# Thirty-two unrolled batch tiles rewritten as a hardware loop of eight iterations, in a kernel that stores at the DMA limit

## The chip, the cores and the metric

The kernel runs on one core of one Trainium2 chip. The metric is the device time of one execution in microseconds (us), given as the median of several runs. One execution of each kernel also leaves a trace; its span is the time from the first to the last recorded instruction, 1.8 us less than that execution's device time in the kernel before (1339.7 against 1341.49 us).

## The reference

A batch of 4096 rows, each of 32 fields of 64 numbers. For each of the 496 pairs of fields (i < j), field i goes through the pair's own 64x64 matrix and is multiplied by field j, element by element. The output has 4096 x 31,744 fp32 numbers, 520 MB.

```python
i_idx, j_idx = np.triu_indices(32, k=1)
vi = inputs[:, i_idx, :]                     # inputs (4096, 32, 64)
vj = inputs[:, j_idx, :]
vdotw = jnp.einsum('bpd,pde->bpe', vi, W)    # W (496, 64, 64)
return (vdotw * vj).reshape(4096, -1)
```

## The kernel before

A batch tile is 128 rows, one on each partition. Its x is loaded and transposed on TensorE (PE), so that a field's 64 numbers lie on partitions and PE loads them as weights ahead of the matmuls with that field's matrices (the trace has 4,864 such loads of 64x128, 194 ns each, and as many matmuls of 64x512 or less, 559 ns each on average). The products of PE land in one of four PSUM slots; VectorE (DVE) multiplies them by x and writes the result into a ring in SBUF; SyncE (SP) issues one store for each of five groups of fields. The weights stay in SBUF. The 32 batch tiles are unrolled by a Python loop, so each instruction is executed once.

```python
STORES = [[0, 1], [2, 3], [4, 5], [6, 7, 8], [9, 10, 11, 12, 13, 14, 15]]
PREFETCH_AT = [5, 6]
RING = 28160
...
for p in range(NPR):                          # 16 loads of weights, issued by SP
    wp = const.tile([P, width[2 * p]], F32, tag=f"w{p}", name=f"w{p}")
    nc.sync.dma_start(out=wp, in_=w[:, woff[p] : woff[p] + width[2 * p]])
    w_sb.append(wp)
... # transpose x of tile 0
for t in range(NT):                           # 32 batch tiles
    xt, xT = xs.pop(t), xTs.pop(t)
    if t + 1 < NT:
        xs[t + 1] = load_x(t + 1)             # issued by ACT
    for s, group in enumerate(STORES):
        if at + store_w[s] > RING:
            at = 0
        osb = ring[:, at : at + store_w[s]]
        at += store_w[s]
        for p in group:
            ... # transposes of the next x tile at p = 5 and 6
            for c0 in range(0, width[2 * p], BANK):
                pm = psum.tile([P, 2, BANK], F32, tag="ps")        # 4 slots in turn
                ... # two matmuls into pm, then one or two DVE products into osb
        nc.sync.dma_start(out=out[ts(t, P), o0 : o0 + store_w[s]], in_=osb)
```

## Time and profile before

| | before |
|---|---|
| time | 1341.44 us (1341.24 to 1341.58, in the rounds with the changed kernel) |
| span, instructions executed | 1339.7 us, 13,755 |
| DMA | 9 in all slices but the last, 420 GB/s over the span |
| DVE, PE busy | 88%, 86% |
| DVE's first product, first store issued | 13.16 us, 24.61 us |

The lines that carry this stand in the prediction. In the page a digit is the busy share of one of 40 slices in tenths; a queue's line gives packets, megabytes and share of sixteen DMA engines; a line of the waits gives who waits for whom, microseconds in total, how often, and the longest.

### The profile page before, as it was taken

How to read it: one execution, taken by the hardware profiler on the slowest of the kernel's cores; microseconds unless marked ns; L12 is line 12 of the kernel's file. 1: busy time of each engine (PE TensorE's matmuls, PEld its weight loads, DVE VectorE, ACT ScalarE, POOL GpSimd, SP SyncE). 2: the span in 40 equal slices, each digit the busy share in tenths (PEclk: the TensorE clock that was granted, in tenths of full speed). 3: DMA queues.
4: the chain of work that ended last, by engine and by line, in shares of the span. 5: the costliest groups of instructions: out<-in, count | busy, mean ns of one | idle time of the engine just before them, and what ended most of it. 6: DMA issues, size and time to landing. Idle time of an engine off the chain costs nothing.

```text
span 1339.7 us, 13755 instructions
## 1 busy us (share of the span) xinstructions
PE 1151.0 (86%) x5376; PEld 548.7 (41%) x5376; DVE 1177.4 (88%) x1664; ACT 66.1 (5%) x65; POOL 0.7 (0%) x6
## 2 busy tenths in 40 slices
PE   7998889888898888988888978889798897888992
PEld 3444344443343443443433534444344443444441
DVE  6999889888899988989888989899898997898993
ACT  1000000000000000000000000000000000000000
POOL 0000000000000000000000000000000000000000
PEclk9999889999999999989999899899898998998996
DMA  9999999999999999999999999999999999999996
GB/s 392 426 431 434 429 431 429 427 427 434 426 434 430 422 422 430 422 424 429 415 426 424 426 426 404 415 420 431 428 420 408 431 427 431 416 424 420 422 429 264
DMA packets 30017, 562.93 MB, mean 420 GB/s; under 512 B 3456, under 2 KB 3840, under 8 KB 5376
## 3 DMA queue, kind: packets, MB, share of 16 engines
q1 hardware_dynamic: 25344, 528.49, 92.6%
q10 hardware_dynamic: 4608, 33.56, 6.0%
q8 instruction: 42, 0.69, 0.2%
q14 instruction: 23, 0.19, 0.0%
HBM read 41.94 MB, written 520.09 MB: 420 GB/s over the span
## 4 chain that ended last, share of the span: by engine, by line
DMA 54%; DVE 23%; PE 11%; issue 9%; DVEq 0%
DMA out_dram<-ring 54%; DVE ring L130 15%; PE pm L120 9%; DVE ring L139 9%; PE pt L80 2%; DMA x<-in_x_dram 1%; DVEq L130 0%; DVEq L177 0%
## 5 line engine op out<-in xcount | busy, mean ns | idle before, releaser
L120 PE MATMUL pm<-w,xT 64*128 64x512 f32 (+7 forms) x4864 | 1083.2, 559 | 158.3 <-DVE ring L130 140.1
L130 DVE TENSOR_TENSOR ring<-pm,x 128x1024 f32<-128x1024 f32 x768 | 904.0, 1217 | 138.4 <-DMA out_dram<-ring 93.0
L120 PEld LDWEIGHTS pm<-w,xT 64*128 64x128 f32 x4864 | 487.7, 194 | 720.1 <-DVE ring L130 451.3
L139 DVE TENSOR_TENSOR ring<-pm,x 128x448 f32<-128x448 f32 (+6 forms) x896 | 330.2, 415 | 3.6 <-PE pm L120 2.9
L81 ACT COPY xT<-pt 128x1024 f32<-128x1024 f32 x64 | 64.8, 1012 | 1194.6 <-PE pt L80 1194.6
L80 PE MATMUL pt<-ident,x 128*128 128x128 f32 x512 | 76.5, 297 | 8.5 <-DMA x<-in_x_dram 8.5
L80 PEld LDWEIGHTS pt<-ident,x 128*128 128x128 f32 x512 | 61.0, 152 | 48.9 <-issue 35.3
L81 ACT ACT_TABLE_LOAD x1 | 1.3, 1283 | 1.7 <-PEq L173 1.7
masks.py:199 POOL TENSOR_SCALAR_AFFINE_SELECT ident<-ident 128x128 f32<-128x128 f32 x1 | 0.3, 292 | 0.1
masks.py:197 POOL MEMSET ident<- 128x128 f32 x1 | 0.2, 204 | 0.3 <-POOLq L173 0.3
L173 POOL MEMSET const-bfloat16-1.0<- 128x1 bf16 x1 | 0.1, 101 | 0.0
L173 POOL MEMSET const-uint8-127<- 128x1 uint8 x1 | 0.1, 101 | 0.0
L173 POOL MEMSET const-float32-0.0<- 128x1 f32 x1 | 0.1, 98 | 0.2 <-issue 0.2
L173 POOL MEMSET const-float32-1.0<- 128x1 f32 x1 | 0.1, 98 | 0.0
## 6 DMA issues: line engine op xcount, KB each, us to landing
out_dram<-ring SPq DMA_DIRECT2D x32, 3776.0 KB, 22.8
out_dram<-ring SPq DMA_DIRECT2D x32, 3264.0 KB, 21.8
out_dram<-ring SPq DMA_DIRECT2D x32, 3168.0 KB, 22.4
out_dram<-ring SPq DMA_DIRECT2D x32, 2912.0 KB, 22.3
out_dram<-ring SPq DMA_DIRECT2D x32, 2752.0 KB, 22.1
x<-in_x_dram ACTq DMA_DIRECT2D x32, 1024.0 KB, 14.2
w<-in_w_dram SPq DMA_DIRECT2D x1, 992.0 KB, 7.4
w<-in_w_dram SPq DMA_DIRECT2D x1, 928.0 KB, 11.7
```

Source lines behind the costliest of these rows:

```text
L80: nc.tensor.transpose(pt[:, ts(c, P)], xt[:, ts(n * g + c, P)], ident)
L81: nc.scalar.copy(xT[:, ts(g, 2 * BANK)], pt)
L120: nc.tensor.matmul(pm[:, h, : n[h]], xT[h * D : (h + 1) * D, ts(p, P)], w_sb[p][h * D : (h + 1) * D, c0 : c0 + n[h]], start=True, stop=True,)
L130: nc.vector.tensor_tensor(runs(osb, o[0], o[1], n[0]), pm[:, :, : n[0]], runs(xt, xj[0], xj[1], n[0]), ALU.mult,)
L139: nc.vector.tensor_tensor(osb[:, o[h] : o[h] + n[h]], pm[:, h, : n[h]], xt[:, xj[h] : xj[h] + n[h]], ALU.mult,)
L173: nc = bacc.Bacc("TRN2", target_bir_lowering=False, num_devices=1)
```

## The change

The intent is a smaller program: instead of 32 unrolled tiles, eight iterations of four (the prediction says why four). The loop is built with `iteration_sync="reg_based"`: by that name its waits compare with registers, and the trace of the changed kernel has 1,328 register operations on PE and 1,384 on DVE, where the kernel before has none. Stores are declared disjoint, so that rows held in registers create no dependence between them. The last iteration prefetches one x tile too many, for which x gets 128 rows of zeros.

```diff
-RING = 28160
+RING = 26272
+BODY = 4
...
-    psum = ctx.enter_context(tc.tile_pool(name="ps", bufs=4, space=bass.MemoryType.PSUM))
+    pspool = ctx.enter_context(tc.tile_pool(name="ps", bufs=1, space=bass.MemoryType.PSUM))
...
+    xbuf = [const.tile([P, F * D], F32, tag=f"x{k}", name=f"x{k}") for k in range(2)]
+    xTbuf = [const.tile([P, NPR * P], F32, tag=f"xT{k}", name=f"xT{k}") for k in range(2)]
+    slots = [
+        pspool.tile([P, 2, BANK], F32, tag=f"ps{k}", name=f"ps{k}") for k in range(4)
+    ]
...
-    for t in range(NT):
-        xt, xT = xs.pop(t), xTs.pop(t)
-        if t + 1 < NT:
-            xs[t + 1] = load_x(t + 1)
+    def batch_tile(row, k, nxt):
+
+        xt, xT = xbuf[k], xTbuf[k]
+        load_x(nxt, 1 - k)
...
-            nc.sync.dma_start(out=out[ts(t, P), o0 : o0 + store_w[s]], in_=osb)
+            st = nc.sync.dma_start(out=out[bass.ds(row, P), o0 : o0 + store_w[s]], in_=osb)
+
+            tc.declare_no_dep(
+                st.ins, group="stores", across_iterations=True, reason="disjoint outputs"
+            )
+            tc.add_to_no_dep_group("stores", st.ins)
+
+    first_slot = turn["slot"]
+    with tc.For_i(0, B, BODY * P, iteration_sync="reg_based") as r:
+        for j in range(BODY):
+            batch_tile(r + j * P, j % 2, r + (j + 1) * P)
...
+    x = np.concatenate([x, np.zeros((P, F * D), x.dtype)])
```

More of the change, by code (lines that the diff above doesn't have):

```diff
@@ L47, in pair_bilinear_kernel @@
     nc = tc.nc
-    B = x.shape[0]
+    B = out.shape[0]
     NT = B // P
@@ L57, in pair_bilinear_kernel, with slot @@
     const = ctx.enter_context(tc.tile_pool(name="const", bufs=1))
-    xpool = ctx.enter_context(tc.tile_pool(name="x", bufs=2))
-    xtpool = ctx.enter_context(tc.tile_pool(name="xT", bufs=2))
-    psum = ctx.enter_context(tc.tile_pool(name="ps", bufs=4, space=bass.MemoryType.PSUM))
+    pspool = ctx.enter_context(tc.tile_pool(name="ps", bufs=1, space=bass.MemoryType.PSUM))
     ident = const.tile([P, P], F32, tag="ident", name="ident")
     make_identity(nc, ident)
+    ring = const.tile([P, RING], F32, tag="ring", name="ring")
+    xbuf = [const.tile([P, F * D], F32, tag=f"x{k}", name=f"x{k}") for k in range(2)]
[3 more added lines that the diff above has]
+    ]
+    turn = {"slot": 0, "at": 0}
+    def slot():
+        turn["slot"] = (turn["slot"] + 1) % 4
+        return slots[turn["slot"]]
     def runs(tl, a, b, n):
@@ L68, in runs, with load_x, transpose_x @@
         return bass.AP(ap.tensor, ap.offset, [list(ap.ap[0]), [b - a, 2], list(ap.ap[1])])
-    def load_x(t):
-        xt = xpool.tile([P, F * D], F32, tag="x", name=f"x_{t}")
-        nc.scalar.dma_start(out=xt, in_=x[ts(t, P), :])
-        return xt
-    def transpose_x(xT, t, xt, g):
+    def load_x(row, k):
+        nc.scalar.dma_start(out=xbuf[k], in_=x[bass.ds(row, P), :])
+    def transpose_x(k, g):
         n = 2 * BANK // P
-        pt = psum.tile([P, 2 * BANK], F32, tag="ps", name=f"pt_{t}_{g}")
+        pt = slot().rearrange("p a b -> p (a b)")
         for c in range(n):
-            nc.tensor.transpose(pt[:, ts(c, P)], xt[:, ts(n * g + c, P)], ident)
-        nc.scalar.copy(xT[:, ts(g, 2 * BANK)], pt)
-    def new_xT(t):
-        return xtpool.tile([P, NPR * P], F32, tag="xT", name=f"xT_{t}")
-    ring = const.tile([P, RING], F32, tag="ring", name="ring")
-    at = 0
-    xs = {0: load_x(0)}
+            nc.tensor.transpose(pt[:, ts(c, P)], xbuf[k][:, ts(n * g + c, P)], ident)
+        nc.scalar.copy(xTbuf[k][:, ts(g, 2 * BANK)], pt)
+    load_x(0, 0)
     w_sb = []
@@ L94, in pair_bilinear_kernel @@
         w_sb.append(wp)
-    xTs = {0: new_xT(0)}
     for g in range(2):
-        transpose_x(xTs[0], 0, xs[0], g)
-    for t in range(NT):
-        xt, xT = xs.pop(t), xTs.pop(t)
-        if t + 1 < NT:
-            xs[t + 1] = load_x(t + 1)
+        transpose_x(0, g)
+    def batch_tile(row, k, nxt):
+        xt, xT = xbuf[k], xTbuf[k]
+        load_x(nxt, 1 - k)
         for s, group in enumerate(STORES):
-            if at + store_w[s] > RING:
-                at = 0
-            osb = ring[:, at : at + store_w[s]]
-            at += store_w[s]
+            if turn["at"] + store_w[s] > RING:
+                turn["at"] = 0
+            osb = ring[:, turn["at"] : turn["at"] + store_w[s]]
+            turn["at"] += store_w[s]
             o0 = off[2 * group[0]]
             for p in group:
-                if t + 1 < NT and p in PREFETCH_AT:
-                    if t + 1 not in xTs:
-                        xTs[t + 1] = new_xT(t + 1)
-                    transpose_x(xTs[t + 1], t + 1, xs[t + 1], PREFETCH_AT.index(p))
+                if p in PREFETCH_AT:
+                    transpose_x(1 - k, PREFETCH_AT.index(p))
                 for c0 in range(0, width[2 * p], BANK):
-                    pm = psum.tile([P, 2, BANK], F32, tag="ps", name=f"pm_{t}_{p}_{c0}")
+                    pm = slot()
                     n = [max(0, min(BANK, width[2 * p + h] - c0)) for h in range(2)]
@@ L144, in pair_bilinear_kernel @@
                                 )
-            nc.sync.dma_start(out=out[ts(t, P), o0 : o0 + store_w[s]], in_=osb)
+            st = nc.sync.dma_start(out=out[bass.ds(row, P), o0 : o0 + store_w[s]], in_=osb)
[7 more added lines that the diff above has]
+            batch_tile(r + j * P, j % 2, r + (j + 1) * P)
+    assert turn["slot"] == first_slot and turn["at"] + store_w[0] > RING and BODY % 2 == 0
 def kernel(r_inputs, L0_rec_W):
```

## The prediction

The forecast came to 1350 us: 1341.3 + 2.5 (step 3) + 7.5 (step 6) = 1351, and about 1 less for fewer fetches.

> **What bounds the kernel now.** I read the page from the top: the engines, the 40 slices, the DMA queues and the chain. Then I read the waits, the engines in short stretches at both ends, and the groups of instructions.
>
> ```profile
> span 1339.7 us, 13755 instructions
> ...
> PE 1151.0 (86%) x5376; PEld 548.7 (41%) x5376; DVE 1177.4 (88%) x1664; ACT 66.1 (5%) x65; POOL 0.7 (0%) x6
> ...
> DMA  9999999999999999999999999999999999999996
> GB/s 392 426 431 434 429 431 429 427 427 434 426 434 430 422 422 430 422 424 429 415 426 424 426 426 404 415 420 431 428 420 408 431 427 431 416 424 420 422 429 264
> DMA packets 30017, 562.93 MB, mean 420 GB/s; under 512 B 3456, under 2 KB 3840, under 8 KB 5376
> ...
> q1 hardware_dynamic: 25344, 528.49, 92.6%
> q10 hardware_dynamic: 4608, 33.56, 6.0%
> q8 instruction: 42, 0.69, 0.2%
> q14 instruction: 23, 0.19, 0.0%
> ```
>
> No engine is full, but the DMA row is full in 39 of 40 slices, and the queues add up to 98.8% of sixteen engines' span. So bytes set the time. A tile stores 31,744 fp32 words on each of 128 partitions (16.25 MB) and loads 1.05 MB of x, 17.30 MB in all. Without the first and last slice the mean rate is (420 x 40 - 392 - 264) / 38 = 424.8 GB/s, so a tile costs 17.30 MB / 424.8 GB/s = **40.7 us of DMA**.
>
> The groups and the waits show how close the next engine is:
>
> ```profile
> L130 DVE TENSOR_TENSOR ring<-pm,x 128x1024 f32<-128x1024 f32 x768 | 904.0, 1217 | 138.4 <-DMA out_dram<-ring 93.0
> L139 DVE TENSOR_TENSOR ring<-pm,x 128x448 f32<-128x448 f32 (+6 forms) x896 | 330.2, 415 | 3.6 <-PE pm L120 2.9
> ```
> ```profile
> DVE ring L130 <- DMA out_dram<-ring: 93.0, 53, 3.3
> DVE ring L130 <- PE pm L120: 45.4, 52, 13.2
> ```
>
> DVE has 1177.4 / 32 = **36.8 us a tile** and PE 36.0. DVE's longest wait in total, 93.0 us in 53 pieces (2.9 us a tile), is for a store to leave the ring: the consumer holds up the producer, as behind a full pipe. DVE thus has 40.7 - 36.8 = 3.9 us a tile to spare. The second kind of slack is the backlog. A store lands 22.4 us (median) after its issue, while a mean store of 3.25 MB needs 3.25 / 424.8 = 7.7 us of DMA; so about 22.4 - 7.7 = **14.7 us of other transfers** stand ahead of it. A pause of DVE shorter than that doesn't empty the queue.
>
> The ends, in the stretches (microseconds, busy time and count of PE, PEld, DVE, ACT, POOL, clock, DMA share, GB/s):
>
> ```profile
> 0.00:10.00 10.00, 1.53 (x8) 1.56 (x9) 0.00 (x0) 1.28 (x1) 0.70 (x6) 1.00 0.83 316
> 10.00:20.00 10.00, 9.86 (x48) 5.57 (x47) 6.84 (x8) 2.02 (x2) 0.00 (x0) 1.00 1.01 419
> 20.00:30.00 10.00, 9.27 (x38) 3.12 (x38) 10.00 (x13) 0.00 (x0) 0.00 (x0) 1.00 1.05 413
> ```
>
> DMA is full from the first microseconds, first with weights and x, then with stores. The timeline has the first DVE product at 13.16 us and the first store issued at 24.61 us, just when the 8.4 MB of weights and two x tiles, (8.39 + 2.10) / 0.42 = 25 us of DMA, run out. This handover is the fragile place.
>
> [...] 0.88 MB of fetches are 0.2% of DMA time and stop nothing. [...] the trace shows separate waits of 21 ns in DVE's sequencer, hidden under products of 1217 ns.
>
> **The change part by part.**
>
> 1. *Ring 28160 to 26272.* I walked the allocation. Groups are 7552, 6528, 5504, 6336 and 5824 words. With wrap-around at 28160 no group ever ends above 26272, and the positions repeat every four tiles: tile 4 starts at 0 again. So the two rings are identical, with the same 3 or 4 stores between a slot's use and its reuse, and this costs **0**. It is also why the body has four tiles. PSUM keeps four slots in turn: 42 a tile, 168 an iteration, a multiple of four.
>
> 2. *Compute, stores, x loads.* Per tile the same matmuls, products and 5 stores. Declaring stores disjoint only prevents a dependence that register-held rows would create; the unrolled kernel had none. **0**.
>
> 3. *One x tile more.* The last body prefetches the zero padding: 1.05 MB / 424.8 GB/s = **+2.5 us**, on the bound resource. Its 16 transposes (16 x 0.15 us of PE) fit beside other work.
>
> 4. *Register work.* I expect about one register instruction per wait. DVE's sequencer now handles 1664 products and 750 separate waits, 75 a tile. [...] **0** on the path. [...]
>
> 5. *Seven back edges.* [...] For a fetch under load I take the smallest weight load as an upper estimate: 32 KB landed 5.3 us after issue. [...] A pause of 5 us is below the 14.7 us backlog and is earned back within two tiles (3.9 us each). All seven, if exposed, would be 35 us; I count **0**.
>
> 6. *Loop entry.* Straight code lets PE begin when the first weights are in. A loop may instead make each engine wait, before entering, for everything loaded earlier that the body uses. Weights are issued until 0.73 + 22.97 = 23.7 us and the last lands 5.3 us later, at about 29 us. DVE would start about 2.7 us after (13.16 us less the end of the first transposed copy at about 10.5), near 31.5 instead of 13.2, and the first store would go out 11.45 us later, at 43 instead of 24.6. DMA would run dry from about 27 to 43 us, **+15 us**, never regained because DMA is the bound. I give this one chance in two: +7.5 us.
>
> Sum: 1341.3 + 2.5 + 7.5 = 1351; a small credit for fewer fetches (0.88 MB is at most 2.1 us) makes it 1350.
>
> **The rivals.** *A: hidden loop, no entry wait.* For it: the ring waits and the backlog. Time about 1344 us. *B: entry wait.* For it: the first store comes just when loads run out. Against it: waits against the first weight's semaphore could stay in the body. Time about 1359 us. *C: DVE or PE becomes the bound*, by exposed register work on every wait or by coarser waits across the back edge. For it: a margin of only 3.9 us a tile, and DVE's waits on PE. It needs over 3.9 us a tile; at 5 us exposed it would be 32 x 1.1 = +35 us, about 1376 us. *D: edges drain the pipe*, waiting for all outstanding stores: some 22.4 us of landing plus 11.5 us to refill, seven times, over 200 us. [...] *E: faster* by less fetch traffic: at most 2 us. A 2% gain needs 27 us[...].
>
> **Range and chances.** A and B share most of the weight, and the point lies between them. 1340 holds A with the fetch credit, 1372 holds B with some unhidden edges. Slower means above 1368 us: C, D, or B together with edges, 13% in all. Faster has 2%, within 2% has 85%.
>
> **What would show it.** DMA still at 9 in all inner slices, near 425 GB/s, means that the bound holds. Total bytes near 563 to 564 MB, with 33 x loads, show step 3. A first store near 24.6 us means A, near 43 us with a low first slice of GB/s means B. DVE's wait for the ring still near 93 us means that steps 4 and 5 were hidden; if it falls to nothing while DVE waits for issue or PE, C is true. Gaps in all engines every 164 us are the back edges; gaps longer than 15 us with DMA at zero are D. The prediction fails if the loop makes waits coarser than I could see in the diff.

## More of the kernel before

One view that I did not read closely enough before predicting is the last 25 us, in stretches of 5 us (busy time of PE, weight loads, DVE, ACT, GpSimd, then the clock, the DMA share, and GB/s):

```profile
1315.00:1320.00 5.00, 2.82 (x18) 1.85 (x15) 4.46 (x12) 0.00 (x0) 0.00 (x0) 0.93 1.08 464
1320.00:1325.00 5.00, 0.00 (x0) 0.00 (x0) 0.00 (x0) 0.00 (x0) 0.00 (x0) 0.76 0.93 397
1325.00:1330.00 5.00, 0.00 (x0) 0.00 (x0) 0.00 (x0) 0.00 (x0) 0.00 (x0) 0.50 0.55 235
1330.00:1335.00 5.00, 0.00 (x0) 0.00 (x0) 0.00 (x0) 0.00 (x0) 0.00 (x0) 0.50 0.07 28
1335.00:1340.00 5.00, 0.00 (x0) 0.00 (x0) 0.00 (x0) 0.00 (x0) 0.00 (x0) 0.50 0.03 14
```

Compute ends before 1320, and then DMA doesn't stay full until it stops: from 1328 on its share is 0.07, one engine of sixteen, at 28 GB/s. One DMA engine has work left that the others don't have.

## The result, and the profile after

The changed kernel takes **1355.96 us** (median of 4 runs, 1355.73 to 1356.33), against 1341.44 of before on the same chip. A ratio here is the mean time of one kernel's fast runs over that of the other's of the same rounds, so it isn't quite the ratio of the medians. It is 1.0109, with a 95% interval from 1.0091 to 1.0126: slower by 14.5 us, and within 2%.

The page of the kernel after:

```profile
span 1354.2 us, 17418 instructions
...
PE 1155.1 (85%) x5392; PEld 560.6 (41%) x5392; DVE 1178.5 (87%) x1664; ACT 68.1 (5%) x67; POOL 0.7 (0%) x6
...
DMA  8999999999999999999999999999999999999995
GB/s 352 417 427 427 429 428 429 423 434 428 427 431 429 422 417 414 427 425 433 401 420 427 416 434 398 409 427 426 433 404 410 427 423 431 402 396 433 427 432 250
DMA packets 30141, 563.52 MB, mean 416 GB/s; under 512 B 3472, under 2 KB 3856, under 8 KB 5392
...
q14 instruction: 39, 0.32, 0.1%
q8 instruction: 6, 0.10, 0.0%
```

DMA is still the bound, but it moves 416 GB/s, not 420. The first slice fell from 392 to 352 GB/s. The bytes grew by 0.59 MB net: an x tile more (1.05 MB), and 0.46 MB less of fetched instructions (queue 8 went from 42 packets to 6, queue 14 from 23 to 39). 17,418 instructions were executed, 3,663 more than before. Only 34 of these compute (the padding tile's transposes and copies). The others are register, semaphore and branch work: on PE 1,328 register operations of 32 ns, on DVE 1,384 of 40 to 46 ns (medians), the rest on SP, ACT and in semaphore instructions.

The waits of DVE, and its groups:

```profile
DVE ring L135 <- DMA out_dram<-ring: 92.1, 50, 3.4
DVE ring L135 <- PE ps L125: 34.4, 53, 2.2
DVE ring L135 <- SPq L158: 21.9, 1, 21.9
```
```profile
L135 DVE TENSOR_TENSOR ring<-ps,x 128x1024 f32<-128x1024 f32 x768 | 903.0, 1214 | 149.4 <-DMA out_dram<-ring 92.1
L144 DVE TENSOR_TENSOR ring<-ps,x 128x448 f32<-128x448 f32 (+6 forms) x896 | 328.9, 412 | 5.0 <-PE ps L125 4.9
```

DVE waits for the ring as long as before (92.1 against 93.0 us) and its products cost the same. New is one wait of 21.9 us for SP's sequencer, at the start. The stretches of the head and lines of its timeline (start, duration, engine; in brackets what released it):

```profile
10.00:20.00 10.00, 6.03 (x28) 3.61 (x26) 0.00 (x0) 2.02 (x2) 0.00 (x0) 0.98 1.01 422
20.00:30.00 10.00, 6.69 (x26) 3.22 (x28) 8.06 (x9) 0.00 (x0) 0.00 (x0) 0.67 0.78 311
```
```profile
0.75 20.47 SPq L101 DMA_DIRECT2D w<-in_w_dram  x16
...
12.71 3.63 PE L125 MATMUL ps<-w,xT 64*128 64x512 f32 x16 [0.31 <-ACTq L158]
...
21.68 0.34 ACTq L86 DMA_DIRECT2D x<-in_x_dram  x1
21.94 3.48 DVE L135 TENSOR_TENSOR ring<-ps,x 128x1024 f32<-128x1024 f32 x3 [21.94 <-SPq L158]
...
30.57 0.35 SPq L150 DMA_DIRECT2D out_dram<-ring  x1
```

PE enters the loop at 12.71 us, fills its slots and stops. DVE and the second x load start only at 21.7 to 21.9 us. The trace has SP add to the eight semaphores that count the loop's DMAs at 21.3 to 21.8 us, right after its 16th issue of weights, and DVE waits for these. SP's issues take until 21.2 us because they share eight semaphores with the x load: the trace has the eighth weight load, the ninth transfer, wait for the x tile's semaphore until 8.6 us, and each later one for that of an earlier load. So DVE waits for **issues**, not for the last weights to land. The first store leaves at 30.57 us, 6 us later than before, and between 20 and 30 us DMA's share is 0.78 where it was 1.05 (the view counts a packet whole where it starts, so a share can pass 1).

In the tail the lone engine is there again. The last packet lands 19.2 us after the end of DVE's last product (19.0 us before), and the last store's last packet 8.8 us after those of the other engines (10.3 us before):

```profile
1340.00:1345.00 5.00, 0.00 (x0) 0.00 (x0) 0.00 (x0) 0.00 (x0) 0.00 (x0) 0.50 0.25 105
1345.00:1350.00 5.00, 0.00 (x0) 0.00 (x0) 0.00 (x0) 0.00 (x0) 0.00 (x0) 0.50 0.06 28
```

To place the rest of the loss I summed the records of packets. A stretch's DMA work is the sum of its packets' times over sixteen; its idle time is the remainder. From DVE's first product of tile 4 to that of tile 31:

| kernel | tiles 4 to 31, us | DMA work | DMA idle | idle ahead of tile 1 | idle after tile 31 began, to the end of the span |
|---|---|---|---|---|---|
| before | 1108.5 | 1104.9 | 3.6 | 1.3 | 12.3 |
| after | 1115.4 | 1106.2 | 9.2 | 5.3 | 13.3 |

The head lost 4.0 us of DMA. The middle lost 6.9 us, of which 5.6 us is idle DMA; evenly spread, it is 0.25 us a tile. That loss is in no step of the prediction.

**The slow DMA engine.** In the trace a full store has 128 packets, each as long as one partition's row (30,208 bytes in the first group), and sixteen of 4 bytes. Chaining packets end to start at the end of the kernel before gives sixteen rows, one for each DMA engine, with eight of the long packets of each of the last two stores in every row: fifteen of them finish at 1327.8 to 1328.2 us, and one, which has 23 packets left at 1318.3 us where the others have 11, at 1338.4. I took, for each store, the eight packets that land last. From tile 16 on they follow one another, so they are one engine's (80 of 80 stores before, 77 of 80 after); in tiles 0 to 3, where no engine is eight packets late, they are a mixture. In tiles 16 to 31 they take longer than the store's median packet, which is of about 0.95 us: by 24.0 ns before, by 30.1 ns after. This excess is called the slow engine's extra below. Its rise, 6.1 ns on 40 packets a tile, is an estimated 0.24 us a tile, about as much as the middle lost. The engine falls behind by 0.3 to 0.5 us a tile until it is some 10 us late. A store's semaphore rises in sixteen steps, and DVE's 53 waits for the ring in the kernel before end 0.12 us after the last of them, at the median 8.9 us after the fifteenth (50 waits, 0.12 and 8.4 us in the changed kernel). So DVE gets the ring space late, the next store comes late, and the other fifteen engines run dry for a microsecond or two at some stores, from about tile 11 on. These are the idle 3.6 and 9.2 us. Which of the sixteen it is, the records don't tell.

### The profile page after: what moved, and what is told of

Same layout as the page of the kernel before. It is cut to its first block, busy times and chain, and to the rows that moved or that the text cites. A ratio compares the mean times of both kernels' runs of the same rounds, so it can differ in the third digit from the quotient of the medians.

```text
span 1354.2 us, 17418 instructions
## 1 busy us (share of the span) xinstructions
PE 1155.1 (85%) x5392; PEld 560.6 (41%) x5392; DVE 1178.5 (87%) x1664; ACT 68.1 (5%) x67; POOL 0.7 (0%) x6
## 3 DMA queue, kind: packets, MB, share of 16 engines
q1 hardware_dynamic: 25344, 528.49, 91.9%
## 4 chain that ended last, share of the span: by engine, by line
DMA 50%; PE 25%; DVE 13%; issue 8%; DVEq 1%
DMA out_dram<-ring 50%; PE ps L125 22%; DVE ring L135 8%; DVE ring L144 5%; PE ps L93 3%; DVEq L135 1%; DVEq L144 0%; DVEq L196 0%; DVEq L158 0%
## 5 line engine op out<-in xcount | busy, mean ns | idle before, releaser
L125 PE MATMUL ps<-w,xT 64*128 64x512 f32 (+7 forms) x4864 | 1084.6, 561 | 167.5 <-DVE ring L135 152.8
L135 DVE TENSOR_TENSOR ring<-ps,x 128x1024 f32<-128x1024 f32 x768 | 903.0, 1214 | 149.4 <-DMA out_dram<-ring 92.1
L125 PEld LDWEIGHTS ps<-w,xT 64*128 64x128 f32 x4864 | 497.4, 195 | 719.5 <-DVE ring L135 380.8
L144 DVE TENSOR_TENSOR ring<-ps,x 128x448 f32<-128x448 f32 (+6 forms) x896 | 328.9, 412 | 5.0 <-PE ps L125 4.9
L94 ACT COPY xT<-ps 128x1024 f32<-128x1024 f32 x66 | 66.8, 1012 | 1248.7 <-PE ps L93 1211.1
L93 PE MATMUL ps<-ident,x 128*128 128x128 f32 x528 | 79.4, 299 | 8.8 <-DMA x<-in_x_dram 8.8
L93 PEld LDWEIGHTS ps<-ident,x 128*128 128x128 f32 x528 | 63.2, 152 | 51.1 <-issue 34.2
## 6 DMA issues: line engine op xcount, KB each, us to landing
out_dram<-ring SPq DMA_DIRECT2D x32, 3264.0 KB, 21.8
out_dram<-ring SPq DMA_DIRECT2D x32, 2752.0 KB, 21.8
```

The source lines that it names most:

```text
L93: nc.tensor.transpose(pt[:, ts(c, P)], xbuf[k][:, ts(n * g + c, P)], ident)
L94: nc.scalar.copy(xTbuf[k][:, ts(g, 2 * BANK)], pt)
L125: nc.tensor.matmul(pm[:, h, : n[h]], xT[h * D : (h + 1) * D, ts(p, P)], w_sb[p][h * D : (h + 1) * D, c0 : c0 + n[h]], start=True, stop=True,)
L135: nc.vector.tensor_tensor(runs(osb, o[0], o[1], n[0]), pm[:, :, : n[0]], runs(xt, xj[0], xj[1], n[0]), ALU.mult,)
L144: nc.vector.tensor_tensor(osb[:, o[h] : o[h] + n[h]], pm[:, h, : n[h]], xt[:, xj[h] : xj[h] + n[h]], ALU.mult,)
```

## The experiments

All outputs are right. "In the middle" means from tile 4 to tile 31 as above. The runs x1 to x4 shared one set of runs of before (1341.41 us), the next four another (1341.24), the last two a third (1341.23).

### 1. The changed kernel without its loop

```diff
-    with tc.For_i(0, B, BODY * P, iteration_sync="reg_based") as r:
+    for r in range(0, B, BODY * P):
...
-            tc.declare_no_dep( ... )
-            tc.add_to_no_dep_group("stores", st.ins)
```

> The changed kernel with a Python loop instead of the hardware loop (fixed buffers, ring of 26272 and the extra x tile kept; no registers in the waits). Theory L (the loop itself costs: late first product at the entry, and register work near the ring waits): 1344 us, that is before + 2.5 us of x, first store issued near 24.6 us. Rival F (the fixed buffers or the padded input cost, not the loop): 1350 to 1356 us.

1343.45 us, ratio 1.0015 (1.0001 to 1.0029); 13,828 instructions, DVE's first product at 14.2 us, 1108.3 us in the middle with 3.1 us idle. The new ring, fixed buffers, fixed PSUM slots and the x tile together cost 2.0 us. So some 12.5 us come from the loop itself.

### 2. The weights in seven loads

```diff
-    for p in range(NPR):
-        wp = const.tile([P, width[2 * p]], F32, tag=f"w{p}", name=f"w{p}")
-        nc.sync.dma_start(out=wp, in_=w[:, woff[p] : woff[p] + width[2 * p]])
-        w_sb.append(wp)
+    for g in [[0], [1], [2], [3, 4], [5, 6], [7, 8, 9], [10, 11, 12, 13, 14, 15]]:
+        n = sum(width[2 * p] for p in g)
+        wp = const.tile([P, n], F32, tag=f"w{g[0]}", name=f"w{g[0]}")
+        nc.sync.dma_start(out=wp, in_=w[:, woff[g[0]] : woff[g[0]] + n])
+        for p in g:
+            w_sb.append(wp[:, woff[p] - woff[g[0]] : woff[p] - woff[g[0]] + width[2 * p]])
```

> The changed kernel with the weights in 7 loads instead of 16, so that with x there are 8 transfers before the loop and no issue has to wait for an earlier load. Theory E (the first product at 21.9 us waited for the store queue's sequencer, which reached the loop only after its last weight issue at 20.9 us): first product near 13 us, first store near 25 us, total 4 us less, 1352 us. Rival W (the loop waits for the weights to land, however they are issued): first product stays at 20 us or later, total 1356 us.

1351.94 us, ratio 1.0078 (1.0065 to 1.0092), 4.0 us less than the changed kernel. The timeline and the head of this run:

```profile
0.75 3.45 SPq L102 DMA_DIRECT2D w<-in_w_dram  x7
...
14.74 3.49 DVE L137 TENSOR_TENSOR ring<-ps,x 128x1024 f32<-128x1024 f32 x3 [14.74 <-PE ps L127]
```
```profile
20.00:30.00 10.00, 8.87 (x37) 3.22 (x38) 10.00 (x13) 0.00 (x0) 0.00 (x0) 1.00 1.05 438
```

Seven loads and the x load are eight transfers, as many as the changed kernel has semaphores for its loads ahead of the loop; no issue waits for an earlier load now, SP is through its issues at 4.2 us, and DVE, now released by PE, starts at 14.74 us. DMA is full between 20 and 30 us (1.05 against 0.78). The weights land no earlier than in the changed kernel, which shows that the entry waited for SP's issues and not for the landing. The last packet of weights is here at 28.3 us, and in the changed kernel at 28.2. The entry cost 4.0 us. The middle stays at 1115.1 us: the drift has nothing to do with the entry.

### 3. All 32 tiles in one iteration

```diff
-BODY = 4
+BODY = 32
```

> The changed kernel with all 32 tiles in one iteration: register-held waits, no back edge taken. Theory R (the drift of 0.25 us a tile from tile 4 on comes from register work in the waits): 1356 us as with four tiles, drift unchanged. Rival B (the seven back edges cost some 1 us each): about 1349 us, drift gone.

1359.51 us, ratio 1.0136 (1.0120 to 1.0151). The register-held waits stay, and the seven back edges are gone, yet the middle isn't shorter (1116.8 us). Back edges aren't the cause of the drift. This agrees with the trace of the changed kernel, where a compare-and-branch takes 0.216 us on PE, 0.068 on DVE and 0.054 on SP and ACT, no engine stands still at an edge for a fetch (the next recorded instruction comes within 0.3 us of a branch, and every engine executes eight prefetch hints for the branches), and GpSimd, which has nothing to do, runs through its eight iterations in 3.4 us, so no barrier holds it. The time outside the span is 4.2 us in the profiled run (1359.22 - 1355.0) and 1.8 us in the changed kernel. The trace has three instruction fetches after the last instruction, landing until 1359.5 us, which the changed kernel's trace doesn't have; why they come so late isn't known. One thing doesn't fit what follows: this run executes 506 instructions fewer than the changed kernel (16,912), and its span is 0.8 us longer and not shorter.

### 4. The kernel before with the extra x tile

```diff
-        if t + 1 < NT:
+        if True:
...
+    x = np.concatenate([x, np.zeros((P, F * D), x.dtype)])
```

> The kernel before with the extra x tile of zeros loaded and transposed at the end, nothing else. Estimate: +2.5 us (1.05 MB at 424.8 GB/s), 1344 us. If the end is not bound by DMA, or the zeros hide in the tail: 1341.5 us.

1344.00 us, ratio 1.0019 (1.0005 to 1.0033): +2.6 us, where 2.5 were worked out from bytes and rate.

### 5 and 6. Register instructions without a loop

Into the unrolled kernel of experiment 1 goes one register operation for each PSUM slot that is multiplied, in one run on DVE ahead of the product, in the other on PE ahead of the matmuls. It changes no wait: the semaphore instructions of PE and DVE are as many as without.

```diff
+    def bump(eng, reg_):
+        op = (ALU.add, ALU.bitwise_xor)[turn["n"] % 2]
+        ... # held in order by issue_after
+        r_ = eng.reg_alu(reg_, reg_, 3, op)
...
+                    bump(nc.vector, dve_reg)      # the other run: bump(nc.tensor, pe_reg)
```

> The unrolled form of the changed kernel (1343.5 us) with one register instruction put ahead of the products of every PSUM slot on DVE, 40 a tile, and no loop. In the loop DVE has 23 + 20 register instructions a tile of 46 and 40 ns. Theory D (the drift of 0.25 us a tile comes from register work of DVE that shows after ring waits): 1347 to 1351 us, drift like that of the loop. Rival P (it is PE's register work, or the different waits of the loop): 1343.5 to 1344.5 us.

> The unrolled form of the changed kernel (1343.5 us) with one register instruction ahead of the matmuls of every PSUM slot on PE, 40 a tile, as many as the loop has there (41 of 32 ns). Theory P (PE's register work delays the first matmuls after a ring wait): 1347 to 1351 us. Theory D (DVE's) or Q (the waits themselves, not the added instructions): 1343.5 to 1344.5 us.

On DVE 1346.11 us (1.0037, 1.0023 to 1.0051), on PE 1346.41 us (1.0038, 1.0024 to 1.0052): 2.7 and 3.0 us more than without, for 1,284 and 1,288 instructions more. That is some 2.1 to 2.3 ns for an instruction which takes its engine 32 to 46 ns; so about 95% is hidden. Both times fall between what the expectations gave to their theories (1347 to 1351 us) and to the rivals (1343.5 to 1344.5). The comparison is between sets of runs on different chips (1 is on another chip than 5 and 6); the kernel before differed there by 0.2 us, while a ratio's interval is about 1.9 us wide to each side. So 2.7 and 3.0 us rest on the runs' ranges (1343.10 to 1343.59, 1345.97 to 1346.56), and that they differ from each other isn't shown. What is odd is that both engines pay alike, though PE and DVE have different slack (36.0 and 36.8 us of work in a tile's 40.7 us). Idle DMA in the middle rose from 3.1 to 4.2 (DVE) and 4.4 us (PE), and the slow engine's extra from 24.2 to 25.6 and 25.8 ns. Each of the two theories fits its own dose and neither explains why they are equal. That led to the idea of an effect that doesn't pass through PE or DVE at all (experiment 9).

### 7 and 8. Smaller stores

If the other fifteen engines run dry because the ring holds only three or four stores, then seven smaller stores a tile should give the late engine more room. Experiment 7 does this to the kernel of experiment 2, experiment 8 to the kernel before.

```diff
-STORES = [[0, 1], [2, 3], [4, 5], [6, 7, 8], [9, 10, 11, 12, 13, 14, 15]]
+STORES = [[0], [1], [2], [3, 4], [5, 6, 7], [8, 9, 10], [11, 12, 13, 14, 15]]
...
-RING = 26272      # in the loop only
+RING = 28160
```

> The loop with 7 weight loads (1351.9 us) and seven smaller stores a tile in a ring of 28160, so that at least 14784 words stay in flight when a ring slot comes free (12032 before) and the last store is 2880 words (5824 before). Theory S (the drift is DMA running dry for 1 to 1.5 us at certain stores, because a ring wait is followed by too slow a refill): the drift goes and the tail is 3.5 us shorter, 1336 to 1341 us. Rival T (the drift is slower transfers or a per-tile cost of the loop that no slack hides): only the tail is won, about 1348 us.

> The kernel before with the same seven smaller stores a tile, nothing else. Theory S: tail 3.5 us shorter and the 4 us or so of dry DMA between tiles 11 and 30 gone, 1333 to 1337 us. Rival T: the tail alone, about 1338 us. If the smaller stores move fewer bytes per second, 1341 us or more.

Neither brought the gain hoped for: 1355.63 us with the loop (1.0107, 1.0091 to 1.0122), outside both forecasts, and 1344.96 us without (1.0027, 1.0014 to 1.0041), which is the third case that the expectation had named ("move fewer bytes per second"). Without the loop, DMA no longer ran dry in the middle (idle 0 within the error of the sum, which gave -0.5 us), just as hoped. But the work of DMA grew from 1104.9 to 1110.5 us for nearly the same bytes, and ate more than the gain. With the loop, 6.6 us of idle DMA remain, and 123.1 us of DVE's waits for the ring; why it still runs dry there stays open. The expected gain went into slower packets.

### 9. Register instructions on an engine that does nothing

This is the run that decides. GpSimd has no work in the loop, and nobody waits for it there. In the kernel of experiment 2 it gets 240 register operations in each iteration.

```diff
+    pool_reg = nc.gpsimd.alloc_register("pool_count")
+    nc.gpsimd.reg_mov(pool_reg, 1)
...
+        for m in range(240):
+            nc.gpsimd.reg_alu(pool_reg, pool_reg, 3, (ALU.add, ALU.bitwise_xor)[m % 2])
```

> The loop with the weights in seven loads (1351.94 us when it ran, span 1349.6), plus 240 register instructions per iteration on GpSimd, which does nothing else and which nobody waits for: 1920 more are executed, from a loop, so hardly anything more is fetched. Theory N (every executed instruction, on whatever engine, lengthens the packets of the one slow DMA engine, by 2.2 ns in all per instruction): 1920 x 2.2 ns = +4.2 us, about 1356 us; the slow engine's extra per store packet rises from 29.7 to about 33 ns. Rival L (register instructions cost only where they delay DVE or PE): no change, 1351.5 to 1352.5 us, extra stays at 29.7 ns.

**1355.83 us**, ratio 1.0109 (1.0094 to 1.0125), that is 3.9 us more than the 1351.94 us of experiment 2, for 1,925 instructions more: 2.0 ns each. Lines of the page:

```profile
span 1353.7 us, 19262 instructions
...
PE 1154.3 (85%) x5392; PEld 547.4 (40%) x5392; DVE 1179.3 (87%) x1664; ACT 68.1 (5%) x67; POOL 0.9 (0%) x7
...
q8 instruction: 5, 0.08, 0.0%
```

PE and DVE are as busy as in experiment 2 (1152.3 and 1178.8 us there), and the fetches are the same but for one packet, which had been a possible confusion in experiments 5 and 6. So register work doesn't have to delay PE or DVE to cost time. Its place in time agrees too. The trace has GpSimd's operations, which wait for nothing, almost all between 1.5 and 125 us, that is during tiles 0 to 2.

The engine that lands last was 4.6 us late after tile 1 (2.0 in experiment 2, 1.2 to 1.8 in the nine others that I looked at) and 6.0 us after tile 3 (3.4), and tile 4 began 3.4 us later (174.1 against 170.7). In the last store of tile 1 the five packets that land last follow one another, so they are one engine's, and took 926 to 949 ns, where the store's median is 865; in experiment 2 the two that can be told so took 916. In tile 3, when GpSimd has finished, the last five here took 873 to 898 ns, and the four that can be told so there took 884 to 898. The other engines first run dry for over 1 us in tile 7 here, and in tile 11 in experiment 2. From tile 4 to tile 31 both take the same (1115.6 and 1115.1 us), though DMA's idle share of that is 12.6 us here and 9.3 there: once one engine is late, idle time of the others isn't itself the loss. My expectation of 33 ns over all stores was wrong in this: the extra came early, and in tiles 16 to 31 it was 30.1 ns against 29.7.

A second sign is in every run. After DVE's last product hardly any instruction is executed, and the slow engine has two stores left. In eight runs that I looked at, its packets in these two took 1.5 to 7 ns less than the other engines' had: it is then not slow at all. The other engines run out of packets then as well (in the kernel before DMA's share falls from 1.08 to 0.07), so this sign alone would prove little.

### 10. Relieving the slow engine

```diff
+BYPASS = {(9, 0), (20, 0)}
...
-            nc.sync.dma_start(out=out[ts(t, P), o0 : o0 + store_w[s]], in_=osb)
+            cut = [0, 120, P] if (t, s) in BYPASS else [0, P]
+            for a, z in zip(cut, cut[1:]):
+                nc.sync.dma_start(
+                    out=out[t * P + a : t * P + z, o0 : o0 + store_w[s]], in_=osb[a:z]
+                )
```

> The kernel before, with two of its 160 stores (group 0 of tiles 9 and 20) split into partitions 0 to 119 and 120 to 127. If the slow DMA engine is the one that serves the last eight partitions of a full store, [...] the lag of the slow engine (10.3 us at the last store) falls to near 0 after tile 9 and again after tile 20, the lone work at the end of about 10 us shrinks to a few, and the time is 1331 to 1335 us, better than both kernels. If another engine is the slow one, or if its lag costs nothing: 1341 us or a little more, and the lag at the end still about 10 us.

How a split spreads a store over the engines was assumed there and is not shown.

1376.30 us, ratio 1.0252 (1.0229 to 1.0276): 35 us lost with two stores, though the five runs spread from 1368.83 to 1377.71, and the profiled one is 1370.35. The stretch of the first split store, in this run:

```profile
390.00:400.00 10.00, 8.87 (x46) 4.30 (x48) 8.61 (x11) 2.02 (x2) 0.00 (x0) 1.00 1.00 273
```

All engines are busy (1.00) but move 273 GB/s, where the kernel before moved 425 in the same stretch. The median packet of the split store took 1.87 us, against 1.12 us of the same group one tile earlier, and it landed after 35.2 us. (Queue 1 has 25,358 packets in this run and 25,344 in the kernel before, 7 more for each split.) The lag didn't go away: the last store's was 9.6 us. So this split is a bad one; and as its packets were disturbed that much, the run doesn't tell which engine is the slow one.

## Why the prediction was right or wrong

The time lay 6 us above the point, inside the range and in the class with 85%. But that the sum came out near was luck: two errors had opposite signs.

| step | predicted | measured |
|---|---|---|
| 1, 2: ring, buffers, stores | 0 | 0 within 0.6 us (experiment 1 less the x tile) |
| 3: x tile | +2.5 | +2.6 (experiment 4), +2.0 with the new buffers (1) |
| 4: register work | 0 on the path | about +7.7 |
| 5: back edges | 0 | 0 (experiment 3) |
| 6: entry | +15 with one chance in two, so +7.5 | +4.0 (experiment 2) |
| fetches | -1 | not seen; 0.46 MB less is an estimated 1.1 us at 424.8 GB/s |

The 7.7 us are an estimate: 3,663 more instructions at 2.1 ns, the middle of the 2.0 to 2.3 ns of experiments 5, 6 and 9. With the x tile and the entry they make 13.7 to 14.3 of the 14.5 us. Measured as a rest, the loop without its entry costs 8.5 us (experiment 2 less experiment 1), for 3,509 more instructions, which the 2.1 ns make 7.4 us. What the other 1.1 us are stays open: the loop's coarser waits are a rival for them that no run separates, and no run varied the number of semaphore or branch instructions.

**Step 4 failed.** I weighed each register operation against the slack of its own engine, at an assumed time (the trace has medians of 32 ns on PE and 40 to 46 on DVE), and that reasoning held: DVE's waits for the ring are unchanged (92.1 against 93.0 us), and DVE and PE are no bound. The sign that the prediction named for a hidden step 4, a ring wait still near 93 us, was there, and the cost too. "0 on the path" failed because there was another way onto the path, which no step considered. In these runs, the more instructions are executed, on PE, DVE or GpSimd, the longer the packets of one DMA engine take (experiment 3 is the exception), and in this kernel the engine that lands last sets when DVE gets its ring space (0.12 us after the last of a store's sixteen steps). That instructions cost time which neither PE nor DVE executes or waits for is shown by experiment 9. That the slow DMA engine carries it is shown as far as its lateness and its longer packets, in the same tiles as the instructions, go. What links the two isn't shown. Instruction fetch isn't it, since the fetches fell in the loop by 0.46 MB while the extra grew from 24.0 to 30.1 ns. All runs here list a span and a clock, so all were profiled; whether a run without the profiler loses these 7.7 us too isn't shown.

**Step 6 was right in kind and wrong in size.** There is an entry wait. But I had DVE wait until the last weights land, about 29 us, and start at 31.5 us; it waited for SP's last issue and started at 21.94. The first store left at 30.57 us and not at 43, so DMA lost 4.0 us and not 15. (The 2.7 us between the first transposed copy and DVE's start were read wrongly too: 10.45 us is where that copy begins, and it ends at 11.46, so they are 1.7.) Of the two signs named for the first store, 24.6 and 43 us, neither came.

**The backlog was misread.** I took 22.4 us of landing less 7.7 us of its own work as 14.7 us of other transfers ahead. In the second half of the run some 10 us of that is one late engine; the other fifteen have much less ahead of them, and in the middle they run dry now and then. "DMA still at 9 in all inner slices" is true after as well, and hides it: 5.6 us of idle time in 1115 doesn't move a digit. Rival C (DVE or PE as the bound), D (edges that drain) and E (faster) are refuted by the waits, by experiment 3 and by the time; the outcome is rival B at a quarter of its size, plus what no rival named.

## What to carry to other kernels

This hardware loop wasn't free though DVE had 3.9 us a tile to spare: it cost some 12.5 us. So count the instructions that a loop adds (3,663 here), and test them on an idle engine before blaming a busy one (240 an iteration on GpSimd cost 3.9 us). If a loop is entered late, look at who adds to its semaphores first: here, issuing eight transfers ahead of it in place of 17 took 4.0 us back. And when DMA is the bound, read the last stretch of the profile: here its share of 0.07 over the 5 us from 1330 on was one engine that was 10 us behind, and the landing time of a store was that engine's and not the queue's.

None of the kernels tried beats the kernel before. The loop's gain is the program's size; its best form here is that of experiment 2, 0.8% slower.
